# Seven products in place of eight for one more block of two slices, and the last products of layer 0's first pass in another order

## The chip, the cores and the metric

One Trainium2 chip, one NeuronCore. The metric is the device time of one execution in microseconds, as the median of several runs of the same program; lower is better.

## The reference

Four layers follow each other on `x` of shape 8 x 2048 x 64 with one normalised adjacency matrix `adj` of 2048 x 2048. Each is a graph convolution, added to its input and normalised over the 64 features:

```python
x = _layernorm(x + _L0_gnn_ref(x, adj, embedding, weight, bias))   # x, A x, 2 A(A x) - x, weights made per node
x = _layernorm(x + _L1_gnn_ref(x, 0, net_params, adj))             # relu(A z W), twice
x = _layernorm(x + _L2_gnn_ref(x, adj, w_self, w_neigh, bias))     # x Ws + (A x) Wn + b
x = _layernorm(x + _L3_gnn_ref(x, adj, adj, weight, bias))         # x, A x, 2 A(A x) - x, concatenated, times W
```

Nearly all the arithmetic is `A @ z`, with `z` holding 8 batches of 64 features, 512 columns in all. There are seven such products: two in each of layers 0, 1 and 3, and one in layer 2. All data is float32. The change lies in the first of them, `A x` of layer 0.

## The kernel before

`xy` holds two full node arrays in SBUF (slots 0 and 1): 16 node tiles of 128 nodes, each with 512 columns, which are four *pairs* of two batches (128 columns each). Products 2 to 7 (`product`, L216) are Strassen-like at two levels: the 2048 x 2048 matrix is cut into 2 x 2 blocks (A11, A12, A21, A22) and replaced by seven block products with the sums S1 to S4, and `inner` (L237) cuts each block product into seven again. The sums of `adj` that they need are kept in DRAM (`comb`) and are made during product 1, when `adj` is read for the first time.

Product 1 is the stage from 0 to 212 us. It goes over four *slices* `ns` = 0 to 3. A slice has the columns of every 512-row group that belong to one 128-row piece, in four chunks of 1 MB (`slices[ns, j]`, tile `a`, four ring buffers). In a slice:

- `prepare` (L634) is a generator that computes the sums of the slice on VectorE and stores them to `comb` through POOL's DMA queue (L649). `inner(q, ...)` makes four sums of 128x512 (tile `si`, tag "C", four buffers), `outer(...)` makes a block sum as two instructions of 128x1024 (tile `so`, tag "T", three buffers), `put(q, s)` stores an outer and makes its inner sums. Each `yield` is a place where the slice's main function goes on with its own work.
- `plain_slice` (L862) is slice 0. It multiplies directly where sums are not there yet, and uses `two_level` (L818) for A11 and A21. `two_level` is seven products of four calls each with 128 columns, each product copied from PSUM by ScalarE (L836) and closed by two VectorE adds (L847, L850). It needs the four sums of x blocks (`t1[c]`, made by `sums_t`) and four sums of `adj` blocks. `t1[c]` lies in slot 1 of `xy`, in node tiles c, c+4, c+8, c+12, which at that time hold nothing else.
- `fast_slice` (L896) is slices 1 to 3. By the seven-product form it computes the raw A12 block times x (`p2`), A22 by `two_level` (result `q3`), the raw A11 block times x (`pa`, 16 calls of 256 columns, copied to `p1`), then S1, S2, S4 and S3 times their sums of x (`mul`, L914; results `pc`, `pb_`, `pe`; S3 is accumulated onto S2's bank). `done(blk, ps, plus)` (L929) adds two results into the slice's four feature-major results `hT`, one for each pair (tag "t", five buffers, a tag that the weight tile `w3` also uses until `sum_weights` has run).
- `keep_t1` (L780) stores an `hT` to DRAM from SP's queue. `back` (L858) brings it back to node-major form: four TensorE transposes (`to_nodes`, L461), one ScalarE copy into node tiles ns, ns+4, ns+8, ns+12 of slot 1.

Jobs such as `back` and `biases` (L735) are generators in a `Pump` (L28). `mul` calls `pump.step()` once after each of its two halves, and so sets where such a job's instructions stand in TensorE's order. Slice 2's four `back` jobs are held (`held`) until A22 of slice 3 is over, because they overwrite x sums in node tiles 2, 6, 10, 14 that A22 reads. `join_bias` (L766) adds the node bias of layer 0 to a quarter of slot 0, once x itself is no longer needed there; before, it reads the bias from PSUM. After the slices, product 2 reads slot 1: its first half-product `mma` needs pairs 0 and 1. Pairs 2 and 3 of slice 3 come back in the first pump step of product 2 (`last_back`, L1046), and then four `centered` jobs (L1028) of VectorE work.

Instructions within one engine run in order. The order of the program is the order of the calls, except that an instruction not wrapped in `keep_in_program_order` may be issued elsewhere by the scheduler if its inputs are ready.

Of the kernel before, what the change touches and what calls it, by code (L numbers as in the profile page):

```python
# [16 lines left out]
P = 128  # L17
# [87 lines left out]
def kernel(  # L105
# [71 lines left out]

    W1A, W1B, W2N, W2S, W3X, W3A, W3AA = range(7)
    wd = const.tile([P, 7, P], F32, tag="wd", name="wd")

    w3o = const.tile([P, 2, F], F32, tag="w3o", name="w3o")
    w2o = const.tile([P, 2, F], F32, tag="w2o", name="w2o")
    b2 = const.tile([P, F], F32, tag="b2", name="b2")
# [32 lines left out]
    def product(src, feature, between=None, rate=1, own=None, pin=False, runs=None, onto_slot=None, ends=False):  # L216
# [20 lines left out]
        def inner(q, b, finish, early=None, tail=None, next_sum=None, home=None):  # L237
# [13 lines left out]

            t1 = add(new(), b12, b11, ALU.subtract)
            t2 = add(new(), b22, t1, ALU.subtract)
            t3 = add(new(), b22, b12, ALU.subtract)
            t4 = add(new(), b21, t2, ALU.subtract)
            if next_sum is not None and home is None:
# [328 lines left out]
    if True:  # L585
# [8 lines left out]
        def load_weights():  # L594
            nc.gpsimd.memset(wd, 0.0)
            w3 = sums.tile([P, 5, F], F32, tag="t", name="w3", bufs=5)
            for k in range(2):
                half = slice(k * F, (k + 1) * F)
                for i, src in ((W1A, w_l1[0]), (W1B, w_l1[1]), (W2N, w_neigh), (W2S, w_self)):
                    nc.sync.dma_start(wd[half, i, half], src)  # L600
                nc.scalar.dma_start(w3[half], w_l3.rearrange("(k i) o -> i k o", i=F))
            nc.sync.dma_start(b2, b_l2.to_broadcast([P, F]))
            nc.sync.dma_start(b3, b_l3.to_broadcast([P, F]))
            return w3

        def sum_weights(w3):
            pin = tc.keep_in_program_order

            for k in range(2):
                half = slice(k * F, (k + 1) * F)  # L610
                pin(nc.vector.tensor_tensor(wd[half, W3A, half], w3[half, 1], w3[half, 3], ALU.add))
                pin(nc.vector.tensor_tensor(w3[half, 2], w3[half, 2], w3[half, 4], ALU.add))
                pin(nc.vector.tensor_tensor(wd[half, W3X, half], w3[half, 0], w3[half, 2], ALU.subtract))
                pin(nc.vector.tensor_scalar(wd[half, W3AA, half], w3[half, 2], 2.0, None, ALU.mult))


            for k in range(2):
                half = slice(k * F, (k + 1) * F)
                center(wd[half, W2N:, half], half, pin=pin)
            for w in (W2S, W3X):  # L620
                pin(nc.vector.tensor_tensor(wd[:, w, :], wd[:, w, :], ident, ALU.add))
            for k in range(2):
                half = slice(k * F, (k + 1) * F)
                for n, w in enumerate((W3A, W3X)):
                    pin(nc.vector.tensor_copy(w3o[half, n], wd[half, w, half]))
                for n, w in enumerate((W2N, W2S)):
                    pin(nc.vector.tensor_copy(w2o[half, n], wd[half, w, half]))
            center(b2.unsqueeze(1), pin=pin)
            center(b3.unsqueeze(1), pin=pin)
# [4 lines left out]
        def prepare(ns, ch, outers):  # L634
# [26 lines left out]
            def raw(I, J):  # L661
                return [ch[2 * J + b][:, 2 * I + a] for a in range(2) for b in range(2)]
# [21 lines left out]
            outers[A22] = inner(A22, *raw(1, 1))  # L684
            yield
            inner(A12, *raw(0, 1))
            if ns == 0:
# [3 lines left out]
                outers[A21] = inner(None, *raw(1, 0))  # L691
            outers[S1] = s1 = outer(rq(1, 0), rq(1, 1), ALU.add)
            outers[S2] = s2 = outer(sq(s1), rq(0, 0), ALU.subtract)
# [5 lines left out]
            put(S1, s1)  # L699
            yield  # L700
            put(S2, s2)
            if ns:
                inner(A11, *raw(0, 0))
            yield
            if ns:
                outers[S3] = s3 = outer(rq(0, 0), rq(1, 0), ALU.subtract)
                yield
            put(S3, s3)
            if ns == 0:
                yield  # L710
            put(S4, s4)
            yield

        with tc.tile_pool(name="p_n", bufs=4, space=PSUM) as p_n, tc.tile_pool(
            name="p_tn", bufs=2, space=PSUM
        ) as p_tn, tc.tile_pool(name="p_b", bufs=1, space=PSUM) as p_b, tc.tile_pool(
            name="xs", bufs=1
# [9 lines left out]
            for k in range(2):  # L727
                nc.scalar.dma_start(bias0[k * F : k * F + D], b_l0)
            pb = p_b.tile([P, NT, F], F32, tag="pb", name="pb")
            e_tile = small.tile([P, TG, 4, F], F32, tag="sq", name="eT").rearrange("p t b f -> p (t b f)")  # L730
            eT = [e_tile[g // 2 * F : g // 2 * F + D, ts(g % 2, GW)] for g in range(NG)]
# [3 lines left out]
            def biases():  # L735

                for t in (h * NT // 2 + k for k in range(NT // 2) for h in range(2)):
                    g = t // TG
                    tc.keep_in_program_order(nc.tensor.matmul(
                        pb[:, t, :], eT[g][:, ts(t % TG, P)], bias0[g // 2 * F : g // 2 * F + D],  # L740
                        start=True, stop=True,
                    ))
                yield
# [22 lines left out]
            def join_bias(h, c):  # L766
                v = xq(h, c).rearrange("p t h (b f) -> p (t h) b f", f=F)
                bias = pb[:, h * NT // 2 : (h + 1) * NT // 2, :].unsqueeze(2)
                bias = bias.to_broadcast([P, NT // 2, B // 2, F])
                tc.keep_in_program_order(nc.vector.tensor_tensor(v, v, bias, ALU.add))  # L770

# [35 lines left out]
            ]  # L807
            t1 = [[by_tiles(xy[:, 1, c:NT:TG, ts(n, 2 * F)]) for n in range(4)] for c in range(2)]
            b4 = [T[3][:, 2 * j : 2 * j + 2, :, ts(p, 2 * F)] for j in range(2) for p in range(2)]
# [86 lines left out]
            def fast_slice(ns, ch, held, rest):  # L896
# [16 lines left out]

                def mul(ps, a, b, start=True, steps=2):  # L914

                    for p in range(2):
                        for k in range(NT // 2):
                            nc.tensor.matmul(  # L918
                                ps[:, ts(p, GW // 2)], b(k, p), a(k // TG, k % TG),
                                start=(start and p == k == 0), stop=(k == NT // 2 - 1),  # L920
                                skip_group_check=True,
                            )
                        if p < steps:
                            pump.step()
                    return ps
# [17 lines left out]

                next(parts)
                for _ in rest:
                    pass
# [7 lines left out]
                load_chunks(ns + 1, 2, 3)  # L954
                for job in held:
                    pump.add(back(*job))
                next(parts)
                pa = mul(bank(), raw(0, 0), x_of(0, 0))
                p1 = sums.tile([P, GW], F32, tag="p1", name="p1")
                nc.scalar.copy(p1, pa)  # L960
                nc.vector.tensor_tensor(q3, q3, p1, ALU.add)
# [13 lines left out]
                nc.vector.tensor_tensor(u2, pc, u2, ALU.add)  # L975
                nc.vector.tensor_tensor(p1, pc, p1, ALU.add)
                next(parts)
                pe = mul(bank(), summed(S4), x_of(1, 1))
                done(1, pe, u2)
                if ns == TG - 1:  # L980
                    join_bias(1, 0)
                mul(pb_, summed(S3), t_of(3), start=False)

                done(2, pb_, q3)
                done(3, pb_, p1)
                return [hT[p] for p in range(NP)]

            last_pairs = []
            for ns in range(TG):
                ch = [chunks.pop((ns, j)) for j in range(NG)]  # L990
                if ns == 0:
# [15 lines left out]
                    hT = next(first4)  # L1007
                    next(parts)
# [5 lines left out]
                for p in range(NP):  # L1014
                    keep_t1(ns, p, hT[p])

                held = []
                for p in range(NP):
                    if ns == TG - 2:
                        held.append((ns, p, hT[p]))  # L1020
                    elif ns == TG - 1 and p >= NP // 2:
                        last_pairs.append(hT[p])
                    else:
                        pump.add(back(ns, p, hT[p]))
# [241 lines left out]
```

## Time and profile before

| | before |
|---|---|
| median of 3 runs | 1666.93 us (1666.32 to 1666.95) |
| profiled execution | 1666.76 us |
| its span, first to last instruction | 1665.0 us |
| granted TensorE clock | 0.999 |
| TensorE busy | 1656.7 us |
| VectorE busy | 965.9 us |
| slice 1 (first raw product to the next slice's) | 58.96 to 111.09 us |
| slice 2 | 111.09 to 160.54 us |
| slice 3 and the last transposes | 160.54 to 211.71 us |

The profile is one execution with its engines' instructions; TensorE appears as PE (matmuls) and PEld (weight loads), VectorE as DVE, ScalarE as ACT, GpSimd as POOL, SyncE as SP. A line of it names the source line, the engine, the operation, `out<-in` and shapes. Idle time in front of an instruction stands in square brackets with what ended it. An f32 matmul call appears as two records, so 16 calls are x32. The ends of matmuls are modelled, so durations of single ones overlap and the start-to-start distance is the cost.

### The profile page before, as it was taken

How to read it: one execution, taken by the hardware profiler on the slowest of the kernel's cores; microseconds unless marked ns; L12 is line 12 of the kernel's file. 1: busy time of each engine (PE TensorE's matmuls, PEld its weight loads, DVE VectorE, ACT ScalarE, POOL GpSimd, SP SyncE). 2: the span in 40 equal slices, each digit the busy share in tenths (PEclk: the TensorE clock that was granted, in tenths of full speed). 3: DMA queues.
4: the chain of work that ended last, by engine and by line, in shares of the span. 5: the costliest groups of instructions: out<-in, count | busy, mean ns of one | idle time of the engine just before them, and what ended most of it. 6: DMA issues, size and time to landing. Idle time of an engine off the chain costs nothing.

```text
span 1665.0 us, 21271 instructions
## 1 busy us (share of the span) xinstructions
PE 1656.7 (100%) x8414; PEld 1060.6 (64%) x8414; DVE 965.9 (58%) x1737; ACT 276.0 (17%) x810; POOL 246.1 (15%) x332
## 2 busy tenths in 40 slices
PE   9999999999999999999999999999999999999998
PEld 5988844444444444444454455599998455579998
DVE  5986895656456456655434365873668344453657
ACT  0200110242142144430010011220001011100001
POOL 1221200254155056550000000000000000000000
PEclk9999999999999999999999999999999999999999
DMA  8998899504503600019877867657888866678884
GB/s 318 340 383 310 316 322 326 200 26 162 205 26 129 250 26 26 26 65 364 290 266 278 304 254 257 229 218 272 291 297 299 306 209 233 230 264 294 316 311 167
DMA packets 81074, 391.56 MB, mean 235 GB/s; under 512 B 8944, under 2 KB 25584, under 8 KB 41040
## 3 DMA queue, kind: packets, MB, share of 16 engines
q1 hardware_dynamic: 68288, 346.78, 58.2%
q0 software_dynamic: 11248, 42.08, 6.7%
q10 hardware_dynamic: 1440, 1.35, 0.3%
q8 instruction: 67, 1.10, 0.3%
q14 instruction: 31, 0.25, 0.0%
HBM read 339.85 MB, written 50.33 MB: 234 GB/s over the span
## 4 chain that ended last, share of the span: by engine, by line
PE 95%; DVE 3%; DMA 1%; issue 0%; SPq 0%; DVEq 0%
PE y L1109 20%; PE mmb L277 17%; PE mma L277 12%; PE mmc L277 12%; PE mmb L270 9%; PE ps_n L918 7%; PE mma L270 6%; PE mmc L270 6%; PE z L1161 3%; PE z L1190 2%; PE ps_i L832 1%; DVE si L640 1%; DMA xy<-in_x 1%; PE pt L1152 1%; DMA bias<-in_b_l 0%; DVE so L640 0%
## 5 line engine op out<-in xcount | busy, mean ns | idle before, releaser
L277 PE MATMUL mmb<-a,t 128*128 128x512 f32 x648 | 292.0, 593 | 0.0
L1119 DVE SCALAR_TENSOR_TENSOR xy<-y,e_sb,xy 128x128 f32<-128x128 f32 x512 | 179.6, 351 | 141.2 <-PE y L1109 125.3
L277 PEld LDWEIGHTS mmb<-a,t 128*128 128x128 f32 x648 | 121.5, 190 | 145.3 <-issue 143.5
L1128 POOL TENSOR_TENSOR s<-s 128x512 f32<-128x512 f32 (+2 forms) x192 | 157.4, 820 | 333.0 <-ACT s L1123 322.8
L1123 ACT ACTIVATE s<-y,e_sb 128x128 f32<-128x128 f32 x512 | 139.3, 383 | 231.5 <-PE y L1109 231.5
L228 DVE TENSOR_TENSOR u<-mmb,p 128x512 f32<-128x512 f32 x84 | 57.9, 689 | 176.5 <-PE mmb L277 121.1
L270 PE MATMUL mmb<-t,a 128*128 128x128 f32 x1344 | 156.9, 275 | 0.0
L270 PEld LDWEIGHTS mmb<-t,a 128*128 128x128 f32 x1344 | 153.5, 192 | 0.0
L1109 PE MATMUL y<-wn,xT 64*128 64x512 f32 x512 | 131.5, 590 | 0.0
L1109 PE MATMUL y<-wn,C 64*128 64x512 f32 x512 | 131.2, 589 | 0.0
L1109 PE MATMUL y<-wn,tT 64*128 64x512 f32 x512 | 131.2, 589 | 0.0
L277 PE MATMUL mma<-a,T 128*128 128x512 f32 x256 | 115.5, 594 | 0.0
L277 PE MATMUL mmc<-a,t 128*128 128x512 f32 x216 | 97.3, 592 | 0.0
L295 ACT COPY p<-mma 128x512 f32<-128x512 f32 x42 | 24.7, 588 | 405.8 <-PE mma L277 248.4
L1109 PEld LDWEIGHTS y<-wn,xT 64*128 64x128 f32 x512 | 49.3, 187 | 61.2 <-issue 60.7
L1109 PEld LDWEIGHTS y<-wn,tT 64*128 64x128 f32 x512 | 49.6, 187 | 60.2 <-issue 60.2
L1109 PEld LDWEIGHTS y<-wn,C 64*128 64x128 f32 x512 | 49.5, 187 | 60.3 <-issue 60.3
L277 PE MATMUL mma<-a,xy 128*128 128x512 f32 x192 | 86.6, 594 | 0.3 <-PE pt_n L465 0.3
L277 PEld LDWEIGHTS mma<-a,T 128*128 128x128 f32 x256 | 47.6, 190 | 56.8 <-issue 56.5
L228 DVE TENSOR_TENSOR C<-mmc,C 128x512 f32<-128x512 f32 x48 | 33.2, 692 | 85.9 <-PE mmc L277 75.1
L277 PEld LDWEIGHTS mmc<-a,t 128*128 128x128 f32 x216 | 40.0, 190 | 45.4 <-issue 45.2
L277 PEld LDWEIGHTS mma<-a,xy 128*128 128x128 f32 x192 | 36.0, 190 | 44.4 <-issue 43.8
(160 smaller groups left out, 2127.5 us busy)
## 6 DMA issues: line engine op xcount, KB each, us to landing
a<-comb SPq DMA_DIRECT2D x240, 1024.0 KB, 4.8
a<-in_blocks SPq DMA_DIRECT2D x54, 1024.0 KB, 4.8
comb<-si POOLq DMA_DIRECT2D x28, 1024.0 KB, 6.2
a<-in_slices SPq DMA_DIRECT2D x15, 1024.0 KB, 9.0
comb<-so POOLq DMA_DIRECT2D x15, 512.0 KB, 9.6
t1T<-hT SPq DMA_DIRECT2D x16, 256.0 KB, 4.6
xT<-in_xT SPq DMA_DIRECT2D x16, 256.0 KB, 3.0
tT<-t1T SPq DMA_DIRECT2D x16, 256.0 KB, 3.1
```

The costliest lines, as they stand in the source:

```text
L228: nc.vector.tensor_tensor(out, a, b, op)
L270: nc.tensor.matmul(to, a[:, k, m, :], xb[:, m, :], start=(start and opens and m == 0), stop=(m == TG - 1), skip_group_check=True,)
L277: nc.tensor.matmul(ps, xb[:, m, :], a[:, :, m, :], start=(start and m == 0), stop=(m == TG - 1), skip_group_check=True,)
L295: nc.scalar.copy(p1, pa)
L640: tc.keep_in_program_order(nc.vector.tensor_tensor(out, a, b, op))
L918: nc.tensor.matmul(ps[:, ts(p, GW // 2)], b(k, p), a(k // TG, k % TG), start=(start and p == k == 0), stop=(k == NT // 2 - 1), skip_group_ ...
L1109: mm = nc.tensor.matmul(y[:, b, :], terms[n][half, ts(k, P)], wn[half, n, h * DH : (h + 1) * DH, :], start=(n == 0), stop=(n == 2),)
L1119: nc.vector.scalar_tensor_tensor(acc, y[:, :, ts(d, F)], e, acc, ALU.mult, ALU.add)
L1123: nc.scalar.activation(s[:, d], y[:, :, ts(d, F)], AF.Copy, scale=e)
L1128: nc.gpsimd.tensor_tensor(s[:, :n], s[:, :n], s[:, n : 2 * n], ALU.add)
L1161: nc.tensor.matmul(z[:, k, :], aT[:, ts(k, P)], wd[:, w, :], start=(n == 0), stop=(n == len(terms) - 1),)
L1190: nc.tensor.matmul(z[n][:, k], xT[half, ts(k, P)], w[half], start=True, stop=True)
```

## The change

Five things, all in or right after product 1:

1. In slices 1 and 2 the A11 block goes through `two_level` too. Its adjacency sums (`inner(A11, ...)`) and S1's outer move to the front of `prepare` for these slices, ahead of A12; in slice 0, `put(S3)` changes places with `put(S2)`, and one step of slice 0's generator less is taken before slice 1 begins.
2. `t1[0]` must live until slice 2, so the two `t1` change node tiles (`1 - c`). Slice 1's `back` jobs would overwrite `t1[0]`; they are held until slice 2's A11 is over, and one is stepped at once.
3. In slice 3, S3 comes before S4, into a bank of its own; the `back` jobs of pairs 0 and 1 are stepped in the middle of S4, whose bank comes from the pool of the transposes (now four banks).
4. The bias results are copied from PSUM to SBUF (`bias`), `join_bias` reads them there, and `join_bias(1, 1)` moves into the third `centered` job.
5. The weights for layers 2 and 3 are loaded into `w2o` directly and summed over both halves at once; `wd` has three entries for seven.

```diff
-            t1 = add(new(), b12, b11, ALU.subtract)
...
+            pin = tc.keep_in_program_order if places else lambda inst: inst
+            def less(a, b):
+                out = new()
+                pin(nc.vector.tensor_tensor(out, a, b, ALU.subtract))
+                return out
+            t1 = less(b12, b11)
...
         def sum_weights(w3):
+            pin(nc.vector.tensor_tensor(w3o[:, 0], w3[:, 1], w3[:, 3], ALU.add))
+            pin(nc.vector.tensor_tensor(w3[:, 2], w3[:, 2], w3[:, 4], ALU.add))
+            pin(nc.vector.tensor_tensor(w3o[:, 1], w3[:, 0], w3[:, 2], ALU.subtract))
+            pin(nc.vector.tensor_scalar(w3[:, 2], w3[:, 2], 2.0, None, ALU.mult))
+            center(w2o, pin=pin)
+            center(w3o, pin=pin)
+            center(w3[:, 2:3], pin=pin)
             for k in range(2):
                 half = slice(k * F, (k + 1) * F)
...
+                for w in (w2o[half, 1], w3o[half, 1]):
+                    pin(nc.vector.tensor_tensor(w, w, ident[half, half], ALU.add))
+                pin(nc.vector.tensor_copy(wd[half, W3AA, half], w3[half, 2]))
...
             outers[A22] = inner(A22, *raw(1, 1))
             yield
+            if ns in (1, 2):
+                outers[A11] = inner(A11, *raw(0, 0))
+                outers[S1] = s1 = outer(rq(1, 0), rq(1, 1), ALU.add)
+                yield
             inner(A12, *raw(0, 1))
...
-            outers[S1] = s1 = outer(rq(1, 0), rq(1, 1), ALU.add)
+            if ns not in (1, 2):
+                outers[S1] = s1 = outer(rq(1, 0), rq(1, 1), ALU.add)
...
             put(S1, s1)
             yield
+            if ns == 0:
+                put(S3, s3)
+                yield
             put(S2, s2)
-            if ns:
+            if ns > 2:
                 inner(A11, *raw(0, 0))
...
-            name="p_tn", bufs=2, space=PSUM
-        ) as p_tn, tc.tile_pool(name="p_b", bufs=1, space=PSUM) as p_b, tc.tile_pool(
+            name="p_tn", bufs=4, space=PSUM
+        ) as p_tn, tc.tile_pool(
...
+                pb = [p_tn.tile([P, TG, P], F32, tag="pt", name="pb") for _ in range(2)]
...
+                for h in range(2):
+                    nc.scalar.copy(bias[:, h * NT // 2 : (h + 1) * NT // 2], pb[h])
...
-            t1 = [[by_tiles(xy[:, 1, c:NT:TG, ts(n, 2 * F)]) for n in range(4)] for c in range(2)]
+            t1 = [[by_tiles(xy[:, 1, 1 - c : NT : TG, ts(n, 2 * F)]) for n in range(4)] for c in range(2)]
...
                 next(parts)
+                if ns < 3:
+                    next(parts)
                 for _ in rest:
                     pass
                 next(parts)
...
-                for job in held:
-                    pump.add(back(*job))
+                if ns > 2:
+                    for job in held:
+                        pump.add(back(*job))
                 next(parts)
-                pa = mul(bank(), raw(0, 0), x_of(0, 0))
-                p1 = sums.tile([P, GW], F32, tag="p1", name="p1")
-                nc.scalar.copy(p1, pa)
+                p1 = new_out("p1")
+                if ns < 3:
+                    two_level(
+                        lambda i, j: lambda m: ch[j][:, m, i], outers[A11], b1[0], t1[0], by_blocks(p1)
+                    )
+                else:
+                    pa = mul(bank(), raw(0, 0), x_of(0, 0))
+                    nc.scalar.copy(p1, pa)
+                if ns == 2:
+                    for job in held:
+                        pump.add(back(*job))
+                    pump.step()
...
                 if ns == TG - 1:
+                    nc.vector.tensor_tensor(q3, pb_, q3, ALU.add)
+                    next(parts)
+                    ps3 = mul(bank(), summed(S3), t_of(3))
+                    done(2, ps3, q3)
+                    for p in range(2):
+                        keep_t1(ns, p, hT[p])
+                        pump.add(back(ns, p, hT[p]))
+                    done(3, ps3, u2)
                     join_bias(1, 0)
+                    pe = p_tn.tile([P, TG, P], F32, tag="pt", name="ps_e").rearrange("p t n -> p (t n)")
+                    mul(pe, summed(S4), x_of(1, 1), n=2)
+                    done(1, pe, u2)
...
-                    if ns == TG - 2:
+                    if ns in (1, 2):
                         held.append((ns, p, hT[p]))
...
-            join_bias(1, 1)
             pump.drain()
         def centered(h, c):
+            if h == c == 1:
+                join_bias(h, c)
+                yield
```

More of the change, by code (lines that the diff above doesn't have):

```diff
@@ L176 @@
     make_identity(nc, ident)
-    W1A, W1B, W2N, W2S, W3X, W3A, W3AA = range(7)
-    wd = const.tile([P, 7, P], F32, tag="wd", name="wd")
+    W1A, W1B, W3AA = range(3)
+    wd = const.tile([P, 3, P], F32, tag="wd", name="wd")
+    w2o = const.tile([P, 2, F], F32, tag="w2o", name="w2o")
     w3o = const.tile([P, 2, F], F32, tag="w3o", name="w3o")
-    w2o = const.tile([P, 2, F], F32, tag="w2o", name="w2o")
     b2 = const.tile([P, F], F32, tag="b2", name="b2")
@@ L250, in new @@
                 return sums.tile([P, TG, 2 * F], F32, tag="t", name="t", bufs=5)
-            t1 = add(new(), b12, b11, ALU.subtract)
-            t2 = add(new(), b22, t1, ALU.subtract)
-            t3 = add(new(), b22, b12, ALU.subtract)
-            t4 = add(new(), b21, t2, ALU.subtract)
+            pin = tc.keep_in_program_order if places else lambda inst: inst
[4 more added lines that the diff above has]
+            t1 = less(b12, b11)
+            t2 = less(b22, t1)
+            t3 = less(b22, b12)
+            t4 = less(b21, t2)
             if next_sum is not None and home is None:
@@ L598, in load_weights @@
                 half = slice(k * F, (k + 1) * F)
-                for i, src in ((W1A, w_l1[0]), (W1B, w_l1[1]), (W2N, w_neigh), (W2S, w_self)):
-                    nc.sync.dma_start(wd[half, i, half], src)
+                for to, src in (
+                    (wd[half, W1A, half], w_l1[0]), (wd[half, W1B, half], w_l1[1]),
+                    (w2o[half, 0], w_neigh), (w2o[half, 1], w_self),
+                ):
+                    nc.sync.dma_start(to, src)
                 nc.scalar.dma_start(w3[half], w_l3.rearrange("(k i) o -> i k o", i=F))
@@ L607, in sum_weights @@
             pin = tc.keep_in_program_order
+            pin(nc.vector.tensor_tensor(w3o[:, 0], w3[:, 1], w3[:, 3], ALU.add))
[5 more added lines that the diff above has]
+            center(w3[:, 2:3], pin=pin)
             for k in range(2):
                 half = slice(k * F, (k + 1) * F)
[L611 to L627, printed above, removed]
+                for w in (w2o[half, 1], w3o[half, 1]):
+                    pin(nc.vector.tensor_tensor(w, w, ident[half, half], ALU.add))
+                pin(nc.vector.tensor_copy(wd[half, W3AA, half], w3[half, 2]))
             center(b2.unsqueeze(1), pin=pin)
@@ L707, in prepare @@
                 yield
-            put(S3, s3)
-            if ns == 0:
-                yield
+                put(S3, s3)
             put(S4, s4)
@@ L728 @@
                 nc.scalar.dma_start(bias0[k * F : k * F + D], b_l0)
-            pb = p_b.tile([P, NT, F], F32, tag="pb", name="pb")
-            e_tile = small.tile([P, TG, 4, F], F32, tag="sq", name="eT").rearrange("p t b f -> p (t b f)")
+            e_tile = xs.tile([P, NG // 2 * GW], F32, tag="eT", name="eT")
+            bias = small.tile([P, TG, 4, F], F32, tag="sq", name="bias").rearrange("p t b f -> p (t b) f")
             eT = [e_tile[g // 2 * F : g // 2 * F + D, ts(g % 2, GW)] for g in range(NG)]
@@ L735, in biases @@
             def biases():
[L737 to L742, printed above, removed]
+                pb = [p_tn.tile([P, TG, P], F32, tag="pt", name="pb") for _ in range(2)]
+                pb = [t.rearrange("p t (b f) -> p (t b) f", f=F) for t in pb]
+                for k in range(NT // 2):
+                    for h in range(2):
+                        g = 2 * h + k // TG
+                        tc.keep_in_program_order(nc.tensor.matmul(
+                            pb[h][:, k, :], eT[g][:, ts(k % TG, P)], bias0[h * F : h * F + D],
+                            start=True, stop=True,
+                        ))
+                for h in range(2):
+                    nc.scalar.copy(bias[:, h * NT // 2 : (h + 1) * NT // 2], pb[h])
                 yield
@@ L767, in join_bias @@
                 v = xq(h, c).rearrange("p t h (b f) -> p (t h) b f", f=F)
-                bias = pb[:, h * NT // 2 : (h + 1) * NT // 2, :].unsqueeze(2)
-                bias = bias.to_broadcast([P, NT // 2, B // 2, F])
-                tc.keep_in_program_order(nc.vector.tensor_tensor(v, v, bias, ALU.add))
+                b = bias[:, h * NT // 2 : (h + 1) * NT // 2, :].unsqueeze(2)
+                b = b.to_broadcast([P, NT // 2, B // 2, F])
+                tc.keep_in_program_order(nc.vector.tensor_tensor(v, v, b, ALU.add))
             def load_chunks(ns, *js):
@@ L912, in t_of, with mul @@
                     return lambda k, p: T[n - 1][:, k // 2, k % 2, ts(p, 2 * F)]
-                def mul(ps, a, b, start=True, steps=2):
+                def mul(ps, a, b, start=True, steps=2, n=1):
                     for p in range(2):
@@ L923, in mul @@
                         if p < steps:
-                            pump.step()
+                            pump.step(n)
                     return ps
@@ L975, in fast_slice @@
                 nc.vector.tensor_tensor(u2, pc, u2, ALU.add)
[L976 to L979, printed above, removed]
                 if ns == TG - 1:
-                    join_bias(1, 0)
-                mul(pb_, summed(S3), t_of(3), start=False)
-                done(2, pb_, q3)
-                done(3, pb_, p1)
+                    nc.vector.tensor_tensor(q3, pb_, q3, ALU.add)
[6 more added lines that the diff above has]
+                    done(3, ps3, u2)
+                    join_bias(1, 0)
+                    pe = p_tn.tile([P, TG, P], F32, tag="pt", name="ps_e").rearrange("p t n -> p (t n)")
+                    mul(pe, summed(S4), x_of(1, 1), n=2)
+                    done(1, pe, u2)
+                else:
+                    nc.vector.tensor_tensor(p1, pc, p1, ALU.add)
+                    next(parts)
+                    pe = mul(bank(), summed(S4), x_of(1, 1))
+                    done(1, pe, u2)
+                    mul(pb_, summed(S3), t_of(3), start=False)
+                    done(2, pb_, q3)
+                    done(3, pb_, p1)
                 return [hT[p] for p in range(NP)]
@@ L1007 @@
                     hT = next(first4)
-                    next(parts)
                     w3 = load_weights()
@@ L1013 @@
                     hT = fast_slice(ns, ch, held, parts if ns == 1 else ())
-                for p in range(NP):
+                for p in range(0 if ns < TG - 1 else 2, NP):
                     keep_t1(ns, p, hT[p])
@@ L1018 @@
                 for p in range(NP):
-                    if ns == TG - 2:
+                    if ns in (1, 2):
                         held.append((ns, p, hT[p]))
-                    elif ns == TG - 1 and p >= NP // 2:
+                    elif ns < TG - 1:
+                        pump.add(back(ns, p, hT[p]))
+                    elif p >= 2:
                         last_pairs.append(hT[p])
-                    else:
-                        pump.add(back(ns, p, hT[p]))
-            join_bias(1, 1)
             pump.drain()
         def centered(h, c):
+            if h == c == 1:
+                join_bias(h, c)
+                yield
             v = xy[:, 0, h * NT // 2 : (h + 1) * NT // 2, c * 4 * F : (c + 1) * 4 * F]
```

## The prediction

> **What bounds the kernel now.** I read the page first: busy shares, slices, chain.
>
> ```profile
> PE 1656.7 (100%) x8414; PEld 1060.6 (64%) x8414; DVE 965.9 (58%) x1737; ACT 276.0 (17%) x810; POOL 246.1 (15%) x332
> PE   9999999999999999999999999999999999999998
> DVE  5986895656456456655434365873668344453657
> PE 95%; DVE 3%; DMA 1%; issue 0%; SPq 0%; DVEq 0%
> ```
>
> TensorE is never below nine tenths before the last slice and carries 95% of the chain. An edit pays if it takes TensorE work away or closes a gap in front of TensorE; it costs if it makes TensorE wait. The change sits in the first 212 us, so next I read the TensorE timeline of 58 to 212 us (start, length, tile, idle before; an f32 matmul call leaves two records, a transpose one).
>
> ```profile
> 68.00 1.05 PE L832 MATMUL ps_i<-a,xy 128*128 128x128 f32 x8
> 69.37 1.13 PE L832 MATMUL ps_i<-si,t 128*128 128x128 f32 x8 [0.31 <-DVE si L640]
> 74.80 3.62 PE L918 MATMUL ps_n<-a,xy 128*128 128x256 f32 x16
> ...
> 209.99 1.45 PE L465 MATMUL pt_n<-ident,hT 128*128 128x128 f32 x8
> 211.71 3.67 PE L277 MATMUL mma<-a,xy 128*128 128x512 f32 x8 [0.27 <-PE pt_n L465]
> ```
>
> Only two gaps: slice 1's A22 product waits for its block sums, and the slices' last transposes hold up the next product. For rates I took the pieces of the critical chain:
>
> ```profile
> 118.60 6.25 PE ps_i L832 x56
> 136.53 31.08 PE ps_n L918 x144
> ```
>
> A 128-wide record costs 6.25/56 = 0.1116 us, a 256-wide one 31.08/144 = 0.2158 us. Last, VectorE, which runs without a break from 28.1 to 108 us and could become the limit:
>
> ```profile
> 94.28 0.21 DVE L611 TENSOR_TENSOR wd<-w 64x64 f32<-64x64 f32 x1
> 100.25 0.68 DVE L941 TENSOR_TENSOR u<-ps_n,p 128x512 f32<-128x512 f32 x1
> 111.29 0.76 DVE L934 TENSOR_TENSOR hT<-ps_n,u 128x256 f32<-128x256 f32 x2 [3.31 <-PE ps_n L918]
> ```
>
> The add at 100.25 must read S2's bank before S3 accumulates into it at 104.2; TensorE finished S2 at 97.3, so VectorE was 3 us late, with 3.3 us left. That slack is the thing to watch.
>
> **TensorE work removed.** In slices 1 and 2 A11 times x goes from 16 calls of 256 columns (32 records x 0.2158 = 6.91 us) to seven products of four calls of 128 (56 x 0.1116 = 6.25): -0.66 us a slice, -1.32 in two. The Trainium skill speaks against this ("TensorE: Matmul & The Clock Gate", Back-to-back issue gap): in a stream of weight loads and matmuls the sustained spacing is about 81 ns at 128 columns and 131 ns at 512, so narrow ones are poor value. Its line gives about 98 ns at 256 (an estimate, linear between them): 56 x 81 = 4.5 against 32 x 98 = 3.1 us, a loss of 1.4 us a slice, 2.8 in all, and the whole change would end near 1668.4. The trace has both widths in this very stream, each call with its own weight load, and its cost per column is 0.872 ns against 0.843. I take the trace.
>
> **The gap in slice 1.** A22 took 68.00 to 74.80 = 6.80 us, in slice 2 it took 6.25: 0.55 lost. VectorE computed its sums from 67.81, after S3's inner sums of slice 0. Now slice 0 does S3 instead of S2 in an earlier place, and the two that remain (S2, S4) come behind slice 1's A22, A11 and S1. A22's sums start at 65.28 and its second one is ready near 66.6, before 68.9. I book -0.55.
>
> **The boundary.** S3 ended at 209.99, the transposes of pairs 0 and 1 are 0.43 us a pair (so inside slice 2, 114.55 to 114.98), 0.87 in all, the next product began at 211.71: 0.85 us lost, on VectorE's closing adds, then on the first ScalarE copy (0.59). Now S3 goes ahead of S4 and those transposes stand in the middle of S4, 3.46 us behind S3's end. The adds of blocks 2 and 3 (4 x 0.42 less overlap, 1.4 us) and the copies fit inside S4, so the next product can follow at once: -0.85. What it reads afterwards is less tight as well: the second `t` it needs was ready 0.5 us early; now join_bias(1,1), 2.28 us, stands behind it, and it should be some 2 us early. join_bias goes into the pump in front of the third centring; the same VectorE time, and by 249 us VectorE was idle again, so nothing waits for it. S3's sums must now be there one product sooner: ready at 192.67, S2 ended 196.18, so 3.5 us are left. One add changes its target and none is new. The S4 bank moves to the other PSUM pool, so the new product's banks were let go long before.
>
> **What is moved at no TensorE cost.** Slice 0's transposes go from A11's pump steps to S1's and S2's, slice 1's behind A11 of slice 2: 0.43 us a pair wherever they stand. Biases: the same 16 matmuls, then two ScalarE copies of 128x512, 0.59 each; ScalarE was idle from 59.4 to 69.1 us. Uncovered they would cost 1.2 us. Adding the bias from SBUF: VectorE takes 2.28 us for 128x2048 from PSUM and 2.28 for the SBUF-only sums of x, so nothing. The A11 result is copied in pieces (7 x 0.27) and closed by two adds (0.93) in place of one copy. Weights: 26 small VectorE instructions took 5.97 us (94.28 to 100.25); 20 at the same pace are 4.6. The memset of wd on POOL (0.85 us at the start) shrinks; nobody waits for it.
>
> **VectorE in slice 1, step by step**, since this is where a cost could enter. An inner set of four is 2.54 us (61.15 to 63.69), an outer 2.27. From 65.28: A22 67.8, A11 70.4, S1 72.6, slice 0's S2 and S4 77.7, A12 80.2, S2 and S4 outers 84.75, A22's closing adds 85.7, S1's inner 88.2, A11's closing adds 89.2, q3 89.8, block 0's adds 90.4, S2's inner 93.0, S3's outer 95.2, weights 99.8; the S2 read is done at 100.5. TensorE on the new order: A22 68.00 to 74.25, A11 to 80.50, S1 with two transposed pairs to 88.28, S2 with two to 96.06, S4 to 102.97. Needs are met: A11's sums 70.4 for about 75, S1 72.6 for 80.5, S2 82.5 for 88.3, S4 84.75 for 96.1, S3 95.2 for 103.0, and the S2 read keeps 2.5 us where it had 3.3.
>
> **Waits that are new.** Block 0's adds in slice 1 need hT buffers: five, four held by slice 0's pairs and one by w3. They come free with S1's transposes, at 84.4 and 88.3; VectorE gets there near 89.8. If it came there directly behind A22's closing adds, it would stand for 2.6 us with S1's inner sums and everything else queued behind: still not more than the slack. In slice 2 four pairs are held; one transposed pair directly behind A11 frees what block 0 needs. I take 0, bounds 0 and +1.
> The A11 sums keep one of four C buffers until TensorE is through with it (80.5), no longer only until stored. POOL's stores of such sums in that stretch:
>
> ```profile
> L649 POOL DMA_DIRECT2D comb<-si x1: 754/754/754, 70.7 to 70.7; - x1
> DMA to landing us min/median/max: 6.1/6.1/6.1
> ```
>
> With 6 us each, A12's sums (77.7) find A22's buffer free since 74.3, S4's (75.15) find S3's free since 70.1. POOL's queue issues the same stores, A11's 22 us sooner. On SP's queue the loads of slice 2's chunks wait for S4's and S3's outers: 84.75 and 95.2 instead of 82.2 and 94.3; they took up to 12 us, so about 97 and 107, for 109.9. Two of slice 3's t1T stores go before S4's end; the last two wait for block 1's adds, about 1 us past S4, and the product load queued behind them waits for the first product's end anyway. I take 0, bounds 0 and +3.
>
> **Sum.** -1.32 - 0.55 - 0.85 = -2.72 us. Span 1665.0, profiled execution 1666.76, median 1666.93: the execution shown lies 0.17 below the median. I predict 1666.93 - 2.72 = 1664.2. About 0.2% (3.3 us) is what a measurement of this kernel can tell from no change; this is 0.16%.
>
> **Rivals.**
> All three gains, nothing lost (0.68): 1664.2, own range 1663.6 to 1664.9. For it: no other gap in the timeline, every due time met.
> Part is given back (0.14): VectorE reaches the S2 read 1 to 3 us past its slack, because block 0's adds stand in its queue waiting for transposes, or A22's sums still come too late. 1665 to 1667. For it: VectorE has no idle in slice 1 to absorb anything; against it: smaller weights work, and the 2.5 us.
> Slower (0.11): the C buffers. Once the chunk loads run, the same stores took 10.8 to 15.2 us (issued at 86 to 92). If the rearranged stores from 64 to 80 us land like that, S4's and A12's sums wait in VectorE's strict queue. Each us of it past 2.5 is lost on TensorE before S3; above 5.2 us in all the change is a loss. At 15 us a landing, S4's wait is about 4 us, A12's some 2 more, the next sets again 3 to 5: 10 in all, giving 1664.2 + 7.5 = about 1671.7. Against it: stores at the same pace there took 5.9 to 6.7 us, and the chunk loads start later.
> More than booked (0.07): the new order also removes waits that the trace shows as part of matmul spacing: about 1663.
>
> **How the numbers follow.** Likeliest case 1664.2. Range 1663.2 to 1666.4: the likeliest case, the milder part of the second and some of the fourth. Faster by over 0.2% (under 1663.6): the fourth case and the low edge of the first, 0.12. Slower by over 0.2% (over 1670.3): most of the third, 0.09. The rest, 0.79, within.
>
> **What would show it.** After: ps_i of slices 1 and 2 in runs of 112 records, ps_n with 64 fewer (32 a slice); no wait of ps_i on si near 69 us; slice 1 ends (first raw product of slice 2) near 109.9, slice 2's 158.7, and the first mma starts near 209.0 directly behind ps_e, pt_n standing inside it. Wrong if TensorE shows a wait before S3 of slice 1, if A11's products take over 6.3 us, or if VectorE stands idle between 61 and 100 us on POOL's stores.

## The result and the profile after

The median went from 1666.59 us (20 runs, 1666.22 to 1667.06) to 1663.91 us (20 runs, 1663.44 to 1664.63): -2.68 us. The ratio is 0.9983, 95% interval 0.9977 to 0.9989. Against 1664.2 us foretold, and -2.72 us foretold as a difference, that is close in size; what has to be shown is that it came from the three places named.

The profiled execution of the changed kernel spans 1662.1 us. From its page, the busy times and the chain:

```profile
PE 1654.1 (100%) x8462; PEld 1060.2 (64%) x8462; DVE 965.5 (58%) x1735; ACT 279.9 (17%) x824; POOL 245.3 (15%) x332
...
PE 99%; DMA 1%; DVE 0%; ACTq 0%; issue 0%; DVEq 0%
```

TensorE's busy time fell by 2.6 us, although it has 48 records more: 112 narrow ones came for 64 wide ones. VectorE's part of the chain went from 3% to nothing: the places where the chain had run through its sums are gone. (3% is some 50 us of chain, which before led back from A22's wait at 69 us through VectorE; it is not the time that was gained.) The TensorE timeline of the stage (start, length, tile, idle before):

```profile
58.78 3.62 PE L937 MATMUL ps_n<-a,xy 128*128 128x256 f32 x16
...
67.82 1.05 PE L851 MATMUL ps_i<-a,xy 128*128 128x128 f32 x8
68.71 1.06 PE L851 MATMUL ps_i<-si,t 128*128 128x128 f32 x8
...
74.07 1.06 PE L851 MATMUL ps_i<-a,xy 128*128 128x128 f32 x8
...
80.32 3.62 PE L937 MATMUL ps_n<-so,T 128*128 128x256 f32 x16
...
95.89 13.98 PE L937 MATMUL ps_n<-so,xy 128*128 128x256 f32 x64
109.71 7.07 PE L937 MATMUL ps_n<-a,xy 128*128 128x256 f32 x32
...
158.50 7.07 PE L937 MATMUL ps_n<-a,xy 128*128 128x256 f32 x32
...
201.04 3.62 PE L937 MATMUL ps_e<-so,xy 128*128 128x256 f32 x16
204.50 1.04 PE L474 MATMUL pt_n<-ident,hT 128*128 128x128 f32 x8
205.37 3.62 PE L937 MATMUL ps_e<-so,xy 128*128 128x256 f32 x16
208.83 3.60 PE L286 MATMUL mma<-a,xy 128*128 128x512 f32 x8
```

No bracket is left: TensorE waits for nobody from 58 us on, and the line at 68.71 has lost the wait on `si` that stood at 69.37. A22 now takes 67.82 to 74.07, A11 74.07 to 80.32, 6.25 us each. The transposes (pt_n) stand inside S4 (ps_e), and the next product follows S4 at once. (The 64 records at 95.89 are slice 1's S4 and S3, 32 each, so S3 begins 6.91 us in, at 102.80.) Differences of starts give the length of each slice, and the same table serves for the runs below:

| us | slice 1 | slice 2 | slice 3 to mma | sum |
|---|---|---|---|---|
| before | 52.13 | 49.45 | 51.17 | 152.75 |
| changed | 50.93 | 48.79 | 50.33 | 150.05 |
| e1: A11 wide again | 51.59 | 49.44 | 50.33 | 151.36 |
| e2: S4 before S3 again | 50.93 | 48.79 | 51.17 | 150.89 |
| e3: old sums first | 53.15 | 48.80 | 50.32 | 152.27 |
| e4: 2.5 us more VectorE | 51.06 | 48.79 | 50.33 | 150.18 |
| e5: 7.4 us more VectorE | see text | see text | 50.32 | 152.19 |
| e6: three C buffers | 50.92 | 48.80 | 50.33 | 150.05 |
| e7: two C buffers | 51.18 | 48.79 | 50.33 | 150.30 |
| e8: A11 of slice 3 too | 50.93 | 48.79 | 50.70 | 150.42 |
| e9: e8 with S3's sums earlier | 50.93 | 48.79 | 49.68 | 149.40 |

-1.20, -0.66 and -0.84 make -2.70 us. What lies behind the first `mma` is the same to 0.1 us (1453.3 us before and after). Between single profiles the start of slice 1 moves by more than some of these terms (58.34 to 59.26 us, and for two profiles of the same changed kernel 58.78 and 58.92), so spans of single profiles are not compared here, only lengths of slices: the second profile of the changed kernel has 50.93, 48.79 and 50.33 us again. The whole times of e1, e2 and e3 below cannot by themselves be told from the kernel before (their intervals reach over 1); what these runs show, they show by their slices.

### The profile page after: what moved, and what is told of

Read it like the earlier page. It is cut to its first block, busy times and chain, and to the rows that moved or that the text cites. A ratio compares the mean times of both kernels' runs of the same rounds, so it can differ in the third digit from the quotient of the medians.

```text
span 1662.1 us, 21389 instructions
## 1 busy us (share of the span) xinstructions
PE 1654.1 (100%) x8462; PEld 1060.2 (64%) x8462; DVE 965.5 (58%) x1735; ACT 279.9 (17%) x824; POOL 245.3 (15%) x332
## 3 DMA queue, kind: packets, MB, share of 16 engines
HBM read 339.85 MB, written 50.33 MB: 235 GB/s over the span
## 4 chain that ended last, share of the span: by engine, by line
PE 99%; DMA 1%; DVE 0%; ACTq 0%; issue 0%; DVEq 0%
PE y L1156 20%; PE mmb L286 17%; PE mma L286 12%; PE mmc L286 12%; PE mmb L279 9%; PE ps_n L937 6%; PE mma L279 6%; PE mmc L279 6%; PE ps_i L851 3%; PE z L1208 3%; PE z L1237 2%; PE ps_n L891 1%; PE pt L1199 1%; DMA xy<-in_x 1%; PE ps_e L937 0%; PE pt_n L474 0%
```

## The experiments

**e1: the narrow products alone.** Everything as changed, but A11 of slices 1 and 2 multiplied by 16 wide calls.

```diff
-                if ns < 3:
+                if ns < 0:
                     two_level(
                         lambda i, j: lambda m: ch[j][:, m, i], outers[A11], b1[0], t1[0], by_blocks(p1)
                     )
                 else:
                     pa = mul(bank(), raw(0, 0), x_of(0, 0))
```

> The changed kernel with A11 in slices 1 and 2 multiplied by the 16 wide calls again; its sums, the order on VectorE, the held transposes and slice 3 stay as changed. Theory (narrow products cost less, rate per column as in the trace): slice 1 from 50.93 to 51.6 us, slice 2 from 48.79 to 49.45, slice 3 stays 50.33; total 1.3 us above the changed kernel, about 1.4 us below the kernel before. Rival (the narrow products are worth nothing or cost, as the sustained spacing on the page would have it): slices 1 and 2 unchanged or shorter by up to 1.4 us each.

Measured: slice 1 51.59, slice 2 49.44, slice 3 50.33; the median 1665.41 us, ratio to before 0.9992 (0.9984 to 1.0001). Its TensorE timeline where the slices begin, and the next product:

```profile
58.35 3.62 PE L937 MATMUL ps_n<-a,xy 128*128 128x256 f32 x16
109.94 7.07 PE L937 MATMUL ps_n<-a,xy 128*128 128x256 f32 x32
159.38 7.07 PE L937 MATMUL ps_n<-a,xy 128*128 128x256 f32 x32
209.71 3.60 PE L286 MATMUL mma<-a,xy 128*128 128x512 f32 x8
```

The narrow products are worth 0.66 and 0.65 us. The rival drawn from the sustained spacing in the Trainium skill ("TensorE: Matmul & The Clock Gate", Back-to-back issue gap) is out for these matmuls: by the measured lengths, the narrow form is the cheaper one. What remains of the change without them, 1.39 us in the stage, is the two gaps.

**e2: the boundary alone.** Slice 3 in its old order, all else as changed. With the order, S4's bank goes back to the pool of the products and S3 back onto S2's bank; the stores and `back` jobs of pairs 0 and 1 come behind S3 again.

```diff
-                if ns == TG - 1:
+                if ns == TG:
                     nc.vector.tensor_tensor(q3, pb_, q3, ALU.add)
...
                     done(1, pe, u2)
+                    if ns == TG - 1:
+                        join_bias(1, 0)
                     mul(pb_, summed(S3), t_of(3), start=False)
...
```

> The changed kernel with slice 3's old order: S4, then S3 accumulated onto S2's bank, then the transposes of pairs 0 and 1; all else as changed. Theory (the old boundary gap is the closing adds and the first copy behind the last product): slice 3 with the boundary from 50.33 to 51.2 us, TensorE waits before pt_n and mma are back, total +0.85 us. Rival (the gap was owed to the bias add in front of the product's sums, or to the banks of two pools, both of which stay changed): it comes back by less than 0.3 us.

Measured: slice 3 from 50.33 back to 51.17, +0.84 us; the median 1665.10 us, ratio to before 0.9992 (0.9983 to 1.0001). From the timeline of all engines at the end of S3:

```profile
208.06 1.45 PE L474 MATMUL pt_n<-ident,hT 128*128 128x128 f32 x8
208.26 0.76 DVE L953 TENSOR_TENSOR hT<-ps_n,u 128x256 f32<-128x256 f32 x2 [3.87 <-PE ps_n L937]
208.74 0.53 PEld L474 LDWEIGHTS pt_n<-ident,hT 128*128 128x128 f32 x4 [0.32 <-DVE hT L953]
208.94 0.75 DVE L953 TENSOR_TENSOR hT<-ps_n,p 128x256 f32<-128x256 f32 x2
209.22 1.07 ACT L475 COPY xy<-pt_n 128x512 f32<-128x512 f32 x2 [21.09 <-PE pt_n L474]
209.75 0.30 PEld L286 LDWEIGHTS mma<-a,xy 128*128 128x128 f32 x2 [0.48 <-PE pt_n L474]
209.78 3.67 PE L286 MATMUL mma<-a,xy 128*128 128x512 f32 x8 [0.27 <-PE pt_n L474]
```

The adds start 0.2 us behind the last matmul, and the weight loads of the transposes wait for the first two of them. Then mma's first weight load starts at 209.75. Its bracket names the transposes, but these were done by 209.51. Nor is it the first ScalarE copy, which ends later, at 209.81 (209.22 and 0.59). The last closing add ends at 209.69, and the semaphore records of the trace (counters by which an engine tells others that a step is done) settle it: the wait in front of this weight load is for a counter that VectorE alone raises, and for a load issued 38 us earlier; it ends at 209.73, 0.03 us behind that add. The trace of the kernel before has the same order: last add 211.62, weight load 211.68, end of the first copy 211.74. So the gap is two waits, each for closing adds of S3 on VectorE: that of the transposes, and that of mma, which is about half of it (the last transpose starts at 209.24, takes 0.11, and mma starts at 209.78).

The rival is out: the bias add is not in this chain (here it stands in the pump, as changed), and the pools have their new sizes (four banks and four). Why mma waits for the last add is not shown. By the program it is most likely a bank: that add is the last to read S3's bank, and mma needs one. In the changed kernel S3's adds are over at 202.66 and S4 uses a bank of the other pool, so that mma starts at 208.83, ahead of S4's own adds (209.03). No run has the new order with S4's bank in the old pool, so how much of the 0.84 us the order alone would have won is open.

**e3: the order of VectorE's sums alone.** Slice 0's two remaining inner sums go ahead of slice 1's A22 and A11.

```diff
-                next(parts)
-                if ns < 3:
-                    next(parts)
                 for _ in rest:
                     pass
+                next(parts)
+                if ns < 3:
+                    next(parts)
```

> The changed kernel with slice 0's last inner sums (S2, S4) put ahead of slice 1's A22, A11 and S1 sums on VectorE; the same work in another order. Theory (the due times of A22's sums decide): A22's sums start 5.1 us later, near 70.4, its second sum is there near 71.7, and TensorE, having done the two raw products first, waits about 2 us behind 69.6; everything after moves by that, so slice 1 is 52.9 and the total 2.0 us above the changed kernel. Rival (A22's wait is swallowed by VectorE slack later in the slice): total within 0.5 us of the changed kernel.

Measured: slice 1 53.15, +2.22 us, slices 2 and 3 as they were; the median 1666.00 us, ratio to before 0.9998 (0.9990 to 1.0007): with this order alone most of the gain is gone (2.22 of 2.70 us). The TensorE timeline of A22:

```profile
69.23 1.16 PE L851 MATMUL ps_i<-a,xy 128*128 128x128 f32 x8 [0.40 <-ACT part L855]
71.15 3.31 PE L851 MATMUL ps_i<-si,t 128*128 128x128 f32 x24 [0.76 <-DVE si L647]
```

The first wait comes with another order of TensorE: with the sums late, that order was drawn up anew and puts the two raw products next to each other, on one bank, so that the second waits for the first's copy. The second is the wait for A22's sums. By the starts of the lines, A22 takes 8.47 us (67.78 to 76.25) where it takes 6.25 undisturbed: these are the 2.22 us. No later slack gives it back. The 0.55 us of the kernel before was the same wait with sums half as late.

**e4 and e5: how late VectorE may be.** Two and six instructions of 128x1024 in slice 1, ahead of the weight sums, with the read of S2's bank kept behind them.

```diff
                 if ns == 1:
+                    for _ in range(2):        # e5: 6
+                        tc.keep_in_program_order(nc.vector.tensor_tensor(bias, bias, bias, ALU.max))
                     sum_weights(w3)
...
-                    nc.vector.tensor_tensor(u, a, b, ALU.add)
+                    inst = nc.vector.tensor_tensor(u, a, b, ALU.add)
+                    if ns == 1:
+                        tc.keep_in_program_order(inst)
```

> The changed kernel with two VectorE instructions of 128x1024 more (about 1.15 us each; they leave the bias as it is) ahead of the weight sums of slice 1, and the S2 read kept behind those sums. Theory (slack of the S2 read before S3): the read ends near 102.0, S3 begins at 102.8, so no TensorE wait and slice 1 stays 50.93 us. Rival (VectorE is the bound in slice 1, with no slack): slice 1 grows by about 2.3 us.

> The same with six such instructions, 6.9 us. Theory (past its slack every us of VectorE is a us of TensorE): the S2 read ends near 106.6, S3 waits for it about 3.9 us, slice 1 is 54.8 us, slices 2 and 3 unchanged, and the total is 3.9 us above the changed kernel: a loss against the kernel before. Rival (slack elsewhere takes it, in the next slice or behind S3): slice 1 or the sum of the three slices grows by less than 1 us.

Measured: e4's slice 1 is 51.06, 0.13 us more; its one time was 1664.26 us. In its VectorE timeline, and then in that of the changed kernel, the read is

```profile
102.30 0.68 DVE L960 TENSOR_TENSOR u<-ps_n,p 128x512 f32<-128x512 f32 x1
```

```profile
98.80 0.68 DVE L960 TENSOR_TENSOR u<-ps_n,p 128x512 f32<-128x512 f32 x1
```

In e4 it ends at 102.98 (a us later than foretold); S3 would begin 44.02 us into slice 1 (102.80 - 58.78 in the changed kernel), which is 103.01 here. The read is at its due time to a few hundredths, and the 0.13 us is what that costs: the weight loads of S3 wait 0.3 us for it, until 103.04. That measures the slack: in the changed kernel the read ends at 99.48 for 102.80, 3.3 us ahead.

e5 was half a miss. Its time was 1666.54 us, the stage 152.19 us, +2.14 and not +3.9. VectorE's read and TensorE's order at that place:

```profile
106.74 0.68 DVE L960 TENSOR_TENSOR u<-ps_n,p 128x512 f32<-128x512 f32 x1
```

```profile
103.28 2.32 PE L937 MATMUL ps_n<-a,xy 128*128 128x256 f32 x10
107.48 7.17 PE L937 MATMUL ps_n<-so,xy 128*128 128x256 f32 x32 [1.88 <-DVE u L960]
```

The read ends at 107.42, 4.1 us past S3's due time of 103.28 (59.26 + 44.02); the theory had 3.9. But five calls of slice 2's first raw product (x10, reading chunks only) stand ahead of S3 in this kernel's order, 2.2 us of work, and only the rest is idle. The loss is lateness less what independent work the order puts into the hole.

**e6 and e7: the C buffers.** One and two of four taken away from the start of slice 1 until S2's read. e7 also keeps the wide matmuls in program order.

```diff
+                if ns == 1:
+                    taken = [sums.tile([P, 4, GW], F32, tag="C", name="taken", bufs=4) for _ in range(1)]   # e7: 2
+                    for k in taken:
+                        nc.gpsimd.memset(k[:, 0], 0.0)
...
                 u2 = plus("u2", pb_, p1)
+                if ns == 1:
+                    for k in taken:
+                        nc.gpsimd.tensor_tensor(k[:, 1], u2, k[:, 0], ALU.add)
```

> The changed kernel with one of the four C buffers (the inner sums of adj, held until stored, A11's until TensorE is through with it) taken away from the start of slice 1 until S2's read. Theory (buffers are tight, but the wait falls into VectorE slack): A12's sums wait for A11's buffer, from 77.7 to about 80.4, so VectorE stands 2.6 us; the S2 read ends near 102.1 before S3 begins at 102.8; slice 1 stays 50.9 to 51.1 us, the total within 0.3 us of the changed kernel. Rival (the held A11 buffer is what could make the change slower): slice 1 grows by 2 us or more.

> The same with two of the four C buffers taken away, and the wide matmuls of the slices pinned in program order. Theory: A11's sums wait for S3's store (about 2.3 us), S4's for A11's buffer (about 3 us), A12's for S2's store (about 3 us), some 8 us in all, past the slack of about 3 us; S2's or S3's sums are then late on TensorE, slice 1 is 53 to 56 us and the total 2 to 5 us above the changed kernel, so about as slow as the kernel before or slower. Rival (stores land faster than the buffers are asked for, and the wait is the A11 product alone): slice 1 at most 0.5 us longer.

Measured: slice 1 50.92 in e6 and 51.18 in e7 (times of one run each, 1663.52 and 1663.32 us). Waits on VectorE are there, e6's first, then e7's:

```profile
82.36 0.69 DVE L647 TENSOR_TENSOR si<-a 128x512 f32<-128x512 f32 x1 [4.98 <-DMA comb<-si]
```

```profile
69.22 0.69 DVE L647 TENSOR_TENSOR si<-a 128x512 f32<-128x512 f32 x1 [1.38 <-DMA comb<-si]
...
80.08 0.69 DVE L647 TENSOR_TENSOR si<-so 128x512 f32<-128x512 f32 x1 [3.44 <-PE ps_i L851]
...
83.35 0.69 DVE L647 TENSOR_TENSOR si<-a 128x512 f32<-128x512 f32 x1 [0.65 <-DMA comb<-si]
```

In e6 the wait was 5.0 us, not 2.6: A12's set waited for a store, and not for A11's buffer. TensorE lost nothing all the same. In e7 the waits are the three foretold, for S3's store, for A11's products and for another store, but 5.5 us in sum, not 8, and TensorE lost 0.25 us, not 2 to 5. Further on in e7's VectorE timeline:

```profile
96.69 0.68 DVE L964 TENSOR_TENSOR u<-ps_n,p 128x512 f32<-128x512 f32 x1
...
101.24 2.35 DVE L647 TENSOR_TENSOR so<-a 128x1024 f32<-128x1024 f32 x2
```

The read of S2's bank is at 96.69, amid S2's inner sums and ahead of S3's outer and all the weight sums. It was not kept in program order, so that it left its place behind them, and the slack of about 3 us that e7's theory counted with was no longer the one that mattered. What is then the latest is S3's outer (101.24). In the changed kernel its first half is ready near 94.2, 8.6 us before S3. In e7 it starts 8.7 us later into the slice (42.90 for 34.17): 5.5 us are the waits, 0.6 the read in front, and 2.1 the experiment's own, because two VectorE instructions slow down beside the GpSimd instructions that the edit adds (see the last section). So its slack is just used up, and the weight loads of S3 wait 0.4 us for it. e7 therefore does not show that 8 us of buffer waits would be harmless. With half the buffers gone the change still gains.

**e8 and e9: carried on to slice 3.** A11 of the last slice by seven products too, with the wide matmuls of that slice kept in program order. Its x sums are no longer there (slice 1's transposes lie on them), so they are made again, in `t4` after A22, with S1 moved ahead of A11 for cover.

```diff
-                if ns < 3:
-                    next(parts)
+                next(parts)
...
+                if ns > 2:
+                    sums_t(b1[0], t4)
                 next(parts)
                 p1 = new_out("p1")
+                if ns > 2:
+                    pc = mul(bank(), summed(S1), t_of(1))
+                    next(parts)        # e9 only: S2's inner sums
+                    next(parts)        # e9 only: S3's outer
+                two_level(
+                    lambda i, j: lambda m: ch[j][:, m, i], outers[A11], b1[0], t4 if ns > 2 else t1[0],
+                    by_blocks(p1)
+                )
```

> The changed kernel carried on: slice 3's A11 by seven products as well. Its four x sums are made a second time, in t4 once A22 is over (four more VectorE adds, 2.4 us), S1 goes ahead of A11 to cover them, and A11's and S1's sums come first in slice 3 as they do in slices 1 and 2. TensorE's order in slice 3 is pinned. Theory: slice 3 from 50.33 to 49.67 us, total 0.66 us below the changed kernel, 3.3 below the kernel before. Rival (S3's sums, now later on VectorE, make S3 wait): slice 3 gains nothing or loses up to 1 us, with a TensorE wait in front of S3.

> Slice 3's A11 by seven products, as in the run before it that made S3 wait, with one mend: S2's inner sums and S3's outer are computed while TensorE is in A11, ahead of A11's closing adds, where VectorE stood idle for 5.7 us. Theory (that idle time takes both, 4.8 us, so S3's sums are ready near 185.5 for about 193): no TensorE wait before S3, slice 3 at 49.67 us instead of 50.33 (changed kernel) and 50.70 (without the mend); total 0.66 us below the changed kernel on the same chip. Rival (a buffer of the outers, held by S1 until it is stored, or the delayed closing adds make a new wait before S2 or S3): slice 3 at 50.3 or more.

> The changed kernel itself, beside the next kernel on the same chip, so that the two can be compared directly. Both theories: slices 1, 2, 3 at 50.93, 48.79 and 50.33 us as in its first profile; total 2.7 us below the kernel before; what the start, up to slice 1, takes may differ by a few tenths.

Measured: e8's slice 3 is 50.70, 0.37 us longer than the changed kernel's; the median 1664.63 us, ratio to before 0.9987 (0.9979 to 0.9996). The rival was right. First VectorE's work behind A11 in the changed kernel, then in e8, then e8's TensorE:

```profile
179.87 0.69 DVE L993 TENSOR_TENSOR u<-u,p 128x512 f32<-128x512 f32 x1 [4.16 <-ACT p L987]
```

```profile
186.35 0.56 DVE L864 TENSOR_TENSOR p<-p,part 128x384 f32<-128x384 f32 x1 [5.67 <-ACT p L853]
...
193.28 2.35 DVE L647 TENSOR_TENSOR so<-a 128x1024 f32<-128x1024 f32 x2
```

```profile
194.55 7.17 PE L935 MATMUL ps_n<-so,xy 128*128 128x256 f32 x32 [0.76 <-DVE so L647]
```

S3's outer stands behind the closing adds of A11, and those come 6.3 us later into the slice than q3's add in the changed kernel (27.70 us behind its start, for 21.37); in front of them VectorE is idle for 5.7 us. The 0.66 us are gained and 1.03 lost. e9 uses that idle time:

```profile
183.22 2.36 DVE L647 TENSOR_TENSOR so<-a 128x1024 f32<-128x1024 f32 x2
186.45 0.56 DVE L864 TENSOR_TENSOR p<-p,part 128x384 f32<-128x384 f32 x1 [0.87 <-ACT p L853]
```

and has no TensorE wait before S3; slice 3 is 49.68, -0.65 us. On one chip, the changed kernel's median was 1663.78 us (ratio to before 0.9983, 0.9975 to 0.9992) and e9's 1663.28 us (0.9979, 0.9970 to 0.9988). The intervals overlap; that e9 is the faster one rests on the length of slice 3, with the medians on the same side.

## Why the prediction was right

- **A11 by seven products, -1.32 us:** -1.31 by e1. Rates taken from this very stream held to a hundredth of a us per block (6.25 us).
- **A22's wait, -0.55 us:** slice 1 fell by 1.20 us, of which e1 leaves 0.54 to the wait. The second sum of A22 was foretold for 66.6 and came at 66.70; e3 shows that the order does it.
- **The boundary, -0.85 us:** -0.84 by e2. The size was read off the gap itself and holds. Of the two waits named for it the first, on VectorE's closing adds, is right; the second, on the first ScalarE copy, is not: the next product waited for the last closing add, and started before that copy ended (e2). That the change removes this wait too is owed to S3's earlier place and to S4's bank in the other pool, which the prediction has ("let go long before").
- **The rest at nothing:** slices 2 and 3 show no further difference. Join_bias from SBUF takes 2.28 us as foretold, and its last quarter fits between the centrings.
- **VectorE's walk through slice 1** was right to 0.05 us as far as the end of S3's outer (95.23, foretold 95.2), but for q3's add and block 0's, which changed places. Two terms at its end were off. The weight sums took about 4 us of their own, not 4.6. And the read of S2's bank did not stay behind all of them: it is at 98.80, ahead of the last three, and ended at 99.48 where 100.5 was foretold. The slack grew from 2.5 to 3.3 us (e4), so this error was on the safe side.
- **hT buffers, 0:** block 0's adds ran at 89.16 and 90.09, with VectorE not idle in front of them.
- **The slower rival was priced too high.** It took every us of buffer waits past 2.5 as a us of TensorE. e7 had 5.5 us of such waits and lost 0.25 us; e5 was 4.1 us late and lost 2.1. Its landing times of 15 us were not seen in that stretch (6.0 to 7.6 us in the changed kernel, for the inner sums' stores issued from 64 to 81 us), and in no run did a store of that stretch take over 7.8 us: that case is untested.
- **A sum in the rival on rates:** 1666.93 - 0.55 - 0.85 + 2.8 is 1668.3, not 1668.4. Nothing hangs on it.

The median of before over 20 runs is 0.34 us under that of the three runs shown, which moved the foretold level, not the difference.

## What to carry to other kernels

When one engine is busy throughout, list its gaps with what ends each (where the engine named in a bracket was done earlier, compare the ends of the other candidates, as at 209.75 in e2), and price removed work by the cost per instruction in the same stream; three small terms then add up to what is measured. A step that frees the busy engine moves the due times of everything that others make for it: write the other engine's queue out with times and due times before the move. e8 lost because S3's outer stood in the queue behind adds that were themselves waiting; e9 gained by putting it in front of them. Slack in front of a queue whose order is drawn up again for each kernel can be larger than the old order shows, so a late instruction can cost less than its lateness (e5: 4.1 us late, 2.1 lost).

## What the runs showed of the hardware

**A VectorE instruction that reads what the one directly before it wrote starts about 0.1 us later.** In an inner set of the changed kernel (128x512 each) the second add reads the first one's result and starts 0.72 us behind it (65.29 to 66.01); the third and the fourth read nothing that the one directly before them wrote, and follow after 0.60 and 0.61 us (66.61, 67.22). With 128x1024 it is the same: the six instructions added in e5, each reading and writing the same tile, took 7.43 us from the first to what follows (95.02 to 102.45), 1.24 us each; four outers, none of which reads what the one directly before it wrote, took 4.54 us (80.22 to 84.76 in the changed kernel), 1.14 us each.

**VectorE slowed down beside GpSimd.** In e7 GpSimd ran two adds of 128x512 from 97.53 to 100.77; the two VectorE adds of 128x512 in that time, at 97.89 and 99.57, took 1.75 us each, for 0.69 elsewhere in the same trace. In e6 one small VectorE instruction (the L624 one of the weight sums) took 1.32 us, for 0.20 in e4, while GpSimd's one such add ran (101.01 to 102.28). What the two engines share there, no run shows.
